# Rows of three tiles projected during the second graph; scores in one ring tile, one exponential for two neighbouring chunks

## The chip, the cores and the metric

The kernel runs on one core of a Trainium2 chip. The core has five engines with a queue each: TensorE (PE, matmuls), VectorE (DVE), ScalarE (ACT, activations such as the exponential), GpSimd (POOL) and SyncE (SP, which here only issues DMA transfers). Each engine takes its instructions in the order of its queue and waits at an instruction until what it needs is there. PE writes its results to banks of PSUM; DVE and ACT read them from there.

The metric is the time of one execution on the device in microseconds (us). The profile comes from one execution of its own.

## The reference, cut to what matters

There are 3327 rows of 256 features, which the kernel pads to 3328: 26 tiles of 128 rows. Two layers follow each other. Each layer first adds a graph operation and then a feed-forward part to `x`. The first layer's feed-forward part is a mixture of experts; the second layer's is causal attention with 4 heads (`nh`) and 4 query experts per head (`ne`). The change is in the second layer:

```python
x = x + L1_gnn(layernorm(x), adj, ...)       # the second graph: softmax over neighbours
x = x + L1_ffn(layernorm(x)[None], ...)[0]   # the attention below

sx = einsum('bsh,ndh->bnsd', x, hl_w) + hl_b[None, :, None, :]
pad = sx == 0
q = einsum('bnsd,neod->bneso', sx, wq)
k = einsum('bnsd,nod->bnso', sx, wk)
v = einsum('bnsd,nod->bnso', sx, wv)
scores = einsum('bnesd,bntd->bnest', q, k) * d ** 0.5 + causal
att = softmax(scores, axis=-1)
qkv = einsum('bnest,bntd->bnesd', att, v)
qkv = where(pad[:, :, None], 0.0, qkv)
gs = softmax(einsum('bnsf,nef->bnse', out, gate_w) + gate_b, axis=-1)
mixed = einsum('bnsed,bnse->bnsd', out, gs)
...                                          # residual, two norms, a small network, a gate
```

## The kernel before

The program has three stages one after the other: the first layer (`graph0` and `Experts`), the second graph (`graph1`), and the attention (`heads`). Every instruction is issued through `InOrder`, which keeps the written order on each engine within one function; that is why the profile gives line 61 for almost all of them, and one goes by the names of tiles.

**The second graph** (`graph1`) goes through blocks of 4 tiles of rows, and within a block through 26 steps, one for each tile of neighbours. A step makes weights (`u`, then `p`) on DVE and ACT and adds four matmuls to the accumulators `acc`. At the start of the next block `finish(t)` divides, adds into `x[:, t, :]`, and stores the tile to `xs` in memory with a DMA that POOL issues. So tiles 0 to 3 of `x` are final from the beginning of the second block on. `heads_fixed` spreads the loads of the attention's weights over the steps of the later blocks (`next(fixed, None)`).

**The attention** (`heads`) starts when the second graph ends. Its unit of work is one tile of query rows `t` and one head `h`; the units run through all heads of a tile and then to the next tile. As the attention is causal, unit `(t, h)` covers the keys of tiles 0 to `t`, cut into `t // 4 + 1` chunks `g` of at most 4 tiles (512 keys): 392 chunks in all. For each chunk:

- `fill` (PE): the scores of the 4 experts, `pqk`, from `qt` and `kt`
- `drain` (DVE): copies them from PSUM to `sc`, and takes the maximum of each row on the way (`mx`); after a unit's last chunk `anmax` is the negative maximum over all its chunks
- `weigh` (ACT): `exp(sc + anmax)` for each expert, and the sum of each row into `den`, one column for each chunk
- `turn` (DVE): transposes blocks of 32 x 32 within `sc`
- `values` (SP): loads the chunk's values `vr` from `vs`
- `attend` (PE): `po` collects `sc` times `vr`

When a unit ends, `over` and `back` take `po` out, and after the fourth head a `tail` is put on a list: it computes the gate, the norms and the small network of that tile in many short steps on POOL, ACT, DVE and PE. `tail` sums `den` over its columns.

`prepare(t, res)` makes what a tile needs: it loads `xres` from `xs`, normalizes (`xn`), turns (`xt`), projects (`psxt`, `sxt`), makes the values `v` and stores them to `vs`, then the keys `kt` (`pk`), the queries (`pq`, into `qt`, for the first five tiles `qts`) and `sx`. It is a generator: each `yield` ends a step, and `run(preps)` takes one step for each tile under way. `nz` and `sxd` mark entries of `sx` that are not zero.

The main loop (lines 1503 to 1531) writes out an order by hand: at chunk `k` it drains as far as `wanted(k)` says (through the whole unit that chunk `k + 2`, or `k + 3`, belongs to), attends chunk `k`, turns the next, issues exponentials of chunks up to `k + 2` or `k + 3` (half of the experts before `back`, half after it, but all after it for a unit's first chunk, when its maximum is young), runs steps of `preps` and `tails`, and fills the next chunk. `sc` comes from a pool of 9 buffers of 4 x 512; the queries of the first five tiles take buffers of the same pool.

Of the kernel before, what the change touches and what calls it, by code (L numbers as in the profile page):

```python
# [12 lines left out]
F32 = mybir.dt.float32  # L13
# [4 lines left out]
AF = mybir.ActivationFunctionType  # L18
# [4 lines left out]
P = 128  # L23
# [78 lines left out]
class Net:  # L102
# [378 lines left out]

        return beside

    def graph1(self, xs, made, pool):
        tc, a, x = self.tc, self.a, self.x
        nc = InOrder(tc)
        fixed = self.heads_fixed(pool, nc)
        HP = NP // 2

        PARTS = ((0, HP, HP + 9 * P, NP), (0, HP, NP))  # L490
        with ExitStack() as ctx:
# [125 lines left out]
            first.close()  # L617

            ep = ctx.enter_context(tc.tile_pool(name="g1e", bufs=4))
            abp = ctx.enter_context(tc.tile_pool(name="g1ab", bufs=2))  # L620
            psa = ctx.enter_context(tc.tile_pool(name="g1acc", bufs=8, space=PSUM))
            blocks = [range(i, min(i + 4, NT)) for i in range(0, NT, 4)]
# [123 lines left out]
            weights(0)  # L746
            weights(1)
            masked(0)
            for k, (b, j) in enumerate(steps):

                if b > 2:
                    next(fixed, None)
                if k + 8 in when:
                    load(*when[k + 8])
                if k + 2 < len(steps):
                    if steps[k + 2][1] % 4 == 0 and groups:
                        panel(*groups.pop(0))
                    weights(k + 2)
                if k + 3 in when:
                    sign(*when[k + 3])  # L760
                if k + 1 < len(steps):
                    masked(k + 1)
                gather(k)
                if b and 1 <= j <= len(blocks[b - 1]):
                    finish(blocks[b - 1][j - 1])
                if k in when:
                    top(*when[k], PARTS[1])
                if b + 1 < len(blocks):
                    if j == 16:
                        dg = shifts(b + 1)  # L770
                    if j == 18:
                        pb = rows(b + 1, dg)
                    if j == 21:
                        spread_rows(b + 1, pb)
            for t in blocks[-1]:
                finish(t)


    def heads_fixed(self, one, nc):

# [75 lines left out]
    def heads(self, xs, vs, out):  # L856
# [3 lines left out]
        with ExitStack() as ctx:  # L860
            one = ctx.enter_context(tc.tile_pool(name="at", bufs=1))
            self.work = ctx.enter_context(tc.tile_pool(name="atw", bufs=2))
            scp = ctx.enter_context(tc.tile_pool(name="ats", bufs=9))
            vrp = ctx.enter_context(tc.tile_pool(name="atv", bufs=3))
            tl = ctx.enter_context(tc.tile_pool(name="att", bufs=2))
            sm = ctx.enter_context(tc.tile_pool(name="atsm", bufs=4))
# [5 lines left out]
            )  # L872

            kt = one.tile([P, 4, NP], F32, name="kt")


            load = dict(act=0.0, dve=0.0)
# [29 lines left out]

            def prepare(t, res):

                x = tl.tile([P, D], F32, tag="xres", name="xres", bufs=2)  # L910
                nc.sync.dma_start(out=x, in_=xs[ts(t, P), :])
                yield
# [25 lines left out]
                xt = self.work.tile([P, 2, P], F32, tag="xt", name="xt2", bufs=1)  # L938
                turned(xn, xt)
                yield  # L940
                pp = ps.tile([P, 2, P], F32, tag="b", name="psxt")
                for c in range(2):
                    for k in range(2):
                        nc.tensor.matmul(
                            pp[:, c, :], hlt[:, k, ts(c, P)], xt[:, k, :], start=(k == 0), stop=(k == 1)
                        )
                sxt = self.work.tile([P, 2, P], F32, tag="sxt", name="sxt")
                for c in range(2):
                    nc.scalar.activation(
                        sxt[:, c, :], pp[:, c, :], AF.Identity, bias=hlb[:, c : c + 1]  # L950
                    )
                nz = self.work.tile([P, 2, P], F32, tag="xn", name="nz", bufs=1)
                nonzero(nz, sxt)
                load["act"] += 0.6
                yield

                pp = ps.tile([P, 4, 64], F32, tag="b", name="pv")
                for c in range(2):
                    nc.tensor.matmul(
                        pp[:, 2 * c : 2 * c + 2, :], sxt[:, c, :], wv[:, c, :], start=True, stop=True  # L960
                    )
                v = self.work.tile([P, 4, 64], F32, tag="v", name="v", bufs=1)
                empty(v, pp, D)
                yield

                sxd = self.work.tile([P, 4, P], F32, tag="sxd", name="sxd", bufs=3)
                for k in range(2):
                    for s in range(2):
# [9 lines left out]
                        )  # L978
                for s in range(2):
                    empty(kt[:, s::2, ts(t, P)], pp[s], D)  # L980
                for b in range(4):
                    nc.sync.dma_start(
                        out=vs[:, :, 4 * t + b, :].rearrange("h r d -> r h d"),
                        in_=v[ds(Q * b, Q), :, :],
                    )
                yield
                if t < AHEAD:

                    qt = scp.tile([P, 4, BLK], F32, tag="sc", name="qts")[:, :, : 2 * P]
                    qt = qt.rearrange("p h (i q) -> p h i q", i=2)  # L990
                else:
                    qt = tl.tile([P, 4, 2, P], F32, tag="qt", name="qt")
# [9 lines left out]
                for s in range(2):  # L1002
                    empty(qt[:, s::2, :, :], pp[s], BLK, 8.0)
                yield
                sx = tl.tile([P, D], F32, tag="sx", name="sx", bufs=5)
                turned(sxt.rearrange("p c q -> p (c q)"), sx.rearrange("p (c q) -> p c q", c=2))
                res.update(sx=sx, sxd=sxd, qt=qt)

# [47 lines left out]

            def drain(u, g):

                n = span(u["t"], g)[1] * P
                last = g == u["t"] // 4  # L1060
                if g == 0:
                    u["sc"] = {}
                    u["mx"] = sm.tile([P, 4, 8], F32, tag="mx", name="mx")
                sc = u["sc"][g] = scp.tile([P, 4, BLK], F32, tag="sc", name="sc")
                for e in range(4):
                    s, m = u["pq"][e][:, :n], u["mx"][:, e, g : g + 1]
                    if last:
                        nc.vector.tensor_tensor_reduce(
                            sc[:, e, :n], s, mask[:, BLK - n :], 1.0, NEG, ALU.add, ALU.max, m
                        )  # L1070
                    else:
                        nc.vector.tensor_scalar(
                            sc[:, e, :n], s, 1.0, None, ALU.mult, ALU.max, accum_out=m
                        )
                    load["dve"] += 0.12 + 0.00104 * n
                if last:
                    u["nmax"] = sm.tile([P, 4], F32, tag="nmax", name="anmax")
                    nc.vector.tensor_reduce(
                        u["nmax"], u["mx"][:, :, : g + 1], AX.X, ALU.max, negate=True
                    )  # L1080
                    load["dve"] += 0.2

            def weigh(u, g, experts):

                n = span(u["t"], g)[1] * P
                q = ready[u["t"]]
                if u["h"] == g == 0 and 0 in experts:
                    q["den"] = sm.tile([P, 16, 7], F32, tag="den", name="aden", bufs=3)
                for k in experts:
                    e = u["sc"][g][:, k, :n]  # L1090
                    nc.scalar.activation(
                        e, e, AF.Exp, bias=u["nmax"][:, k : k + 1],
                        accum_out=q["den"][:, 4 * u["h"] + k, g : g + 1],
                    )
                    load["act"] += 0.26 + 0.00088 * n
# [8 lines left out]
            def turn(u, g):  # L1104


                n = span(u["t"], g)[1] * P
                w = u["sc"][g][:, :, :n]
                nc.vector.transpose(w, w)
                load["dve"] += 0.1 + 0.00417 * n  # L1110

# [331 lines left out]
                nc.sync.dma_start(out=out[ts(t, P), :], in_=fo)  # L1443

            units = [dict(t=t, h=h) for t in range(NT) for h in range(4)]
            chunks = [(u, g) for u in units for g in range(u["t"] // 4 + 1)]
            def begin(u):

                t = u["t"]
# [46 lines left out]
            drain_to(wanted(0))  # L1496
            for k in range(2):
                values(*chunks[k])
                weigh(*chunks[k], range(4))
            turn(*chunks[0])  # L1500
            fill_next()
            ended, flipped, weighed = None, 1, 2
            for k, (u, g) in enumerate(chunks):
                drain_to(wanted(k))
                attend(u, g)
# [3 lines left out]
                if k + 2 < len(chunks):  # L1509
                    values(*chunks[k + 2])  # L1510
                rest = []
                while weighed < min(k + 3 + extra(k), len(chunks)):
                    c = chunks[weighed]
                    if c[1]:
                        weigh(*c, range(2))
                    rest.append((*c, range(2 if c[1] else 0, 4)))
                    weighed += 1
                if ended:
                    back(ended)
                last = u if g == u["t"] // 4 else None  # L1520
# [17 lines left out]
class Experts:  # L1538
# [97 lines left out]
    def bank(self):  # L1636
        return self.ps.tile([P, 2, D], F32, tag="r", name="rbank")
# [355 lines left out]
def tile_adj_ffn_d2(ctx: ExitStack, tc: tile.TileContext, a: dict, out: bass.AP):  # L1993
# [5 lines left out]
    with tc.tile_pool(name="feat", bufs=1) as fp:  # L1999
# [4 lines left out]
        with ExitStack() as rows:  # L2004
            with ExitStack() as moe:
                experts = Experts(moe, net, dram, fp)
                net.graph0(experts, weights)
                experts.run(net.graph1_rows(rows))
            net.graph1(xs, experts, ctx.enter_context(tc.tile_pool(name="atf", bufs=1, side="right")))
    net.heads(xs, vs, out)  # L2010


# [76 lines left out]
```

## Time and profile before

| | us |
|---|---|
| median of 3 runs (2863.0 to 2865.1) | 2863.1 |
| the profiled execution | 2863.9 |
| its span, first to last instruction | 2862.2 |
| last `p` of the second graph starts | 961.1 |
| first scores `pqk` of the attention start | 977.9 |
| first maximum `anmax` of tile 1 ends | 1010.5 |
| first maximum of tile 4 ends | 1077.4 |
| first maximum of tile 8 ends | 1248.2 |
| first maximum of tile 16 ends | 1779.9 |
| first maximum of tile 25 ends | 2711.1 |

The attention takes two thirds of the time. Some groups of instructions in it, by form, from 1200 us to the end (count, mean of one in us):

| instruction | count | mean |
|---|---|---|
| ACT exponential of 512, `sc<-sc,anmax` | 946 | 0.713 |
| ACT exponential of 384 | 464 | 0.606 |
| DVE transpose of 4 x 512 | 237 | 2.305 |
| DVE transpose of 4 x 384 | 116 | 1.773 |
| DVE drain of 512, with maximum | 652 | 0.680 |
| DVE drain of 512, with mask and maximum | 288 | 0.680 |

In lines that list instructions in order of time, the columns are: start, duration, engine, line, operation, tile written and tiles read, shapes, how many in a row, and in brackets the idle time of the engine before it with what ended it. `PEld` is the weight load of PE. A chain of waits follows the work that ended last back from the end; its shares are shares of the span.

### The profile page before, as it was taken

What the parts mean: (1) busy time and instruction counts of PE and PEld (TensorE: products, weight loads), DVE (VectorE), ACT (ScalarE), POOL (GpSimd) and SP (SyncE); (2) the same over time, 40 slices, a digit from 0 to 9 for tenths busy, and PEclk for the clock granted to TensorE, in tenths of its full rate; (3) what the DMA queues carried; (4) which work ended last, traced back from release to release, by engine and by line L of the source; (5) the groups of instructions that cost most, each with busy time, mean ns of one, the idle gap of its engine ahead of it and who ended that gap; (6) DMA issues with size and microseconds to landing.
All of it is one profiled execution on the core that took longest, in us unless ns stands there. A gap on an engine that the chain in (4) does not pass through costs nothing.

```text
span 2862.2 us, 125012 instructions
## 1 busy us (share of the span) xinstructions
PE 2665.0 (93%) x53422; PEld 1979.1 (69%) x53422; DVE 2368.9 (83%) x5525; ACT 1790.0 (63%) x5130; POOL 1075.3 (38%) x1562
## 2 busy tenths in 40 slices
PE   7999988878989899999999999999999999999995
PEld 5888877756767666676666666666666666666664
DVE  5203643589999588899999999999999999999996
ACT  6510135555555367777777777777777777777774
POOL 5541644532132137755444333333233222223122
PEclk9999999999999799999999999999999999999998
DMA  9994568657775232333433443434343444434332
GB/s 381 388 337 138 180 217 266 209 183 247 275 273 180 73 94 84 109 108 116 116 111 113 119 121 114 116 118 121 114 127 116 120 120 119 123 116 122 117 107 78
DMA packets 258188, 449.69 MB, mean 157 GB/s; under 512 B 58816, under 2 KB 156608, under 8 KB 257504
## 3 DMA queue, kind: packets, MB, share of 16 engines
q1 hardware_dynamic: 245536, 417.50, 46.0%
q0 software_dynamic: 6576, 18.02, 1.7%
q8 instruction: 420, 6.88, 1.0%
q10 hardware_dynamic: 5520, 6.18, 0.6%
q14 instruction: 136, 1.11, 0.1%
HBM read 393.37 MB, written 25.88 MB: 146 GB/s over the span
## 4 chain that ended last, share of the span: by engine, by line
DVE 35%; PE 28%; ACT 3%; issue 2%; POOL 1%; DMA 0%; SPq 0%; POOLq 0%; DVEq 0%; ACTq 0%
DVE sc L61 32%; PE pqk L61 10%; PE po L61 10%; PE acc L61 2%; ACT sc L61 2%; PE ptO L61 2%; PE psxt L61 1%; PE pt L61 1%; PE pq L61 1%; PE ph L61 0%; ACT sq L61 0%; PE pk L61 0%; PE pv L61 0%; DVE anmax L61 0%; DVE gl L61 0%
## 5 line engine op out<-in xcount | busy, mean ns | idle before, releaser
L61 ACT ACTIVATE sc<-sc,anmax 128x512 f32<-128x512 f32 (+3 forms) x1568 | 1041.4, 669 | 102.9 <-DVE anmax L61 102.9
L61 PEld LDWEIGHTS po<-sc,vr 32*64 32x64 f32 x43728 | 662.5, 131 | 299.1 <-issue 147.6
L61 DVE STREAM_TRANSPOSE sc<-sc 128x2048 f32<-128x2048 f32 (+3 forms) x392 | 816.0, 2082 | 9.7 <-ACT sc L61 9.4
L61 PE MATMUL po<-sc,vr 32*64 32x128 f32 x43728 | 761.1, 276 | 31.6 <-DVE sc L61 21.5
L61 PE MATMUL pqk<-kt,qt 64*128 64x512 f32 (+1 forms) x2944 | 764.4, 585 | 19.0 <-DVE fgs L61 6.6
L61 DVE TENSOR_SCALAR_CACHE_REDUCE sc<-pqk 128x512 f32<-128x512 f32 (+2 forms) x1152 | 653.1, 621 | 26.0 <-PE pqk L61 23.8
L61 PEld LDWEIGHTS pqk<-kt,qt 64*128 64x128 f32 x2944 | 315.9, 185 | 239.5 <-issue 80.9
L61 PE MATMUL acc<-wh,p 128*128 128x259 f32 x1352 | 309.2, 386 | 35.6 <-DVE p L61 35.6
L61 PEld LDWEIGHTS acc<-wh,p 128*128 128x128 f32 x1352 | 253.2, 190 | 93.4 <-DVE p L61 53.3
L61 PE MATMUL acc<-y,pan 128*128 128x256 f32 x1352 | 298.4, 382 | 1.7 <-issue 1.7
L61 ACT ACTIVATION_READ_ACCUMULATOR sc<-sc,anmax 128x1 f32 x1568 | 299.5, 191 | 0.0
L61 PEld LDWEIGHTS acc<-y,pan 128*128 128x128 f32 x1352 | 257.2, 191 | 38.7 <-issue 3.2
L61 POOL TENSOR_TENSOR ot<-ot,sxd 128x512 f32<-128x512 f32 x83 | 105.9, 1276 | 436.2 <-ACT ot L61 431.1
L61 DVE CUSTOM_DVE_ANT_0 sc<-pqk,mask 128x512 f32<-128x512 f32 (+3 forms) x416 | 241.9, 636 | 25.4 <-PE pqk L61 24.6
L61 ACT ACTIVATE u<-u,d 128x512 f32<-128x512 f32 (+1 forms) x182 | 125.2, 688 | 159.2 <-DVE u L61 159.1
L61 DVE SCALAR_TENSOR_TENSOR u<-bc,d 128x512 f32<-128x512 f32 (+1 forms) x182 | 136.0, 748 | 0.1
L61 DVE SCALAR_TENSOR_TENSOR p<-pan,u 128x512 f32<-128x512 f32 (+1 forms) x182 | 126.1, 693 | 10.3 <-PE acc L61 6.1
L61 ACT COPY qkv<-ptO 128x272 f32<-128x272 f32 x104 | 39.7, 381 | 131.0 <-PE ptO L61 130.8
L61 PE MATMUL ptO<-igw,ot 128*128 128x68 f32 x832 | 115.7, 282 | 3.8 <-DVE sc L61 2.1
L61 PEld LDWEIGHTS ptO<-igw,ot 128*128 128x128 f32 x832 | 101.5, 192 | 22.5 <-issue 15.2
L61 ACT ACTIVATE junk<-ar 128x1664 bf16<-128x1664 f32 x52 | 82.8, 1592 | 54.1 <-DMA ar<-in_adj_dram 53.6
L61 DVE CUSTOM_DVE_ANT_0 sg<-sg,dst 128x1664 bf16<-128x1664 bf16 (+2 forms) x56 | 100.1, 1796 | 1.2 <-ACT dst L61 1.0
(356 smaller groups left out, 3082.0 us busy)
## 6 DMA issues: line engine op xcount, KB each, us to landing
vr<-vs SPq DMA_DIRECT2D x976, 128.0 KB
ar<-in_adj_dram SPq DMA_DIRECT2D x104, 832.0 KB
vr<-vs SPq DMA_DIRECT2D x544, 96.0 KB
pan<-in_adjt_dram SPq DMA_DIRECT2D x156, 256.0 KB
pan<-in_adjt_dram SPq DMA_DIRECT2D x26, 1024.0 KB
pan<-in_adjt_dram SPq DMA_DIRECT2D x20, 832.0 KB
w1e<-w SPq DMA_DIRECT2D x59, 256.0 KB
took<-places SPq DMA_DIRECT2D x59, 129.0 KB
```

The source lines that it names most:

```text
L61: made = make(*args, **kw)
```

## The change

It has two parts, and several edits that go with them.

**Rows of tiles 0 to 2.** In `graph1` a new generator `early(t)` runs for tiles 0, 1 and 2, begun at steps 110, 115 and 136 of 182, one of its steps in each step of the graph. It takes `x[:, t, :]` from where it lies, normalizes it (statistics on DVE, the rest on POOL), turns, projects and makes the values, with accumulator banks of `graph1`, and stores the values to `vs`. `sxt` stays in a pool that both functions share, with three buffers. In `heads`, `prepare` of these tiles goes straight to `heads_of`, the part from `nz` and the keys on. `projected`, `valued` and `keep_values` are the former lines of `prepare` as functions. `sx` has 4 buffers in place of 5.

**Scores in a ring, exponentials in pairs.** The pool of 9 buffers becomes one tile `ring` of 4 x (9 x 512), and chunk `c` lies in slot `c % 9` (`c % 6` for the first 24 chunks, while the last three slots hold the queries of the first five tiles). Two neighbouring chunks `g` and `g + 1` of one unit are a pair when `g` is even and they lie in neighbouring slots; a first chunk that is shorter than 512 is then put at the end of its slot, so that the two touch. `weigh` makes one exponential for an expert over both chunks, with one sum, in the column of `g`; `den` is cleared on POOL when a tile begins, because columns of second chunks are no longer written. There are 150 pairs. In the main loop a pair advances `weighed` by two, and a pair that is not a unit's first may be begun one step early, with two of its experts.

```diff
+            def early(t):
+                mv = s.tile([P, 2], F32, tag="mv", name="mv", bufs=6)
+                rs = s.tile([P, 2], F32, tag="rs", name="rs", bufs=6)
+                st = s.tile([P, 6], F32, tag="bnst", name="bnst")
+                nc.vector.bn_stats(st, x[:, t, :])
+                nc.vector.bn_aggr(mv, st)
+                yield
+                nc.gpsimd.tensor_scalar(rs[:, 0:1], mv[:, 1:2], 1e-5, None, ALU.add)
+                nc.gpsimd.tensor_tensor(rs[:, 0:1], rs[:, 0:1], self.nhalf[:, :1], ALU.pow)
+                xn = eap.tile([P, D], F32, tag="xn", name="xn3")
+                nc.gpsimd.tensor_tensor(xn, x[:, t, :], mv[:, 0:1].to_broadcast([P, D]), ALU.subtract)
+                nc.gpsimd.tensor_tensor(xn, xn, rs[:, 0:1].to_broadcast([P, D]), ALU.mult)
+                yield
+                yield
+                pt = bank()
+                for c in range(2):
+                    nc.tensor.transpose(pt[:, c, :], xn[:, ts(c, P)], self.ident)
+                xt = eap.tile([P, 2, P], F32, tag="xt", name="xt3")
+                nc.scalar.copy(xt, pt)
+                yield
+                sxt = pool.tile([P, 2, P], F32, tag="sxt", name="sxt", bufs=3)
+                self.sxts.append(sxt)
+                self.projected(nc, t, bank, sxt, xt)
+                yield
+                pv = self.valued(nc, bank, sxt)
+                v = eap.tile([P, D], F32, tag="v", name="v3")
+                nc.scalar.copy(v.rearrange("p (c q) -> p c q", c=2), pv)
+                self.keep_values(nc, vs, t, v)
+
+            begin = {4 * NT + 6: 0, 4 * NT + 11: 1, 5 * NT + 6: 2}
+            begun = []
             for k, (b, j) in enumerate(steps):
                 if b > 2:
                     next(fixed, None)
+                if k in begin:
+                    begun.append(early(begin[k]))
+                begun = [e for e in begun if next(e, e) is None]
...
             def prepare(t, res):
+                if t < len(self.sxts):
+                    yield from heads_of(t, res, self.sxts[t])
+                    return
...
+            RING = 9
+            ring = one.tile([P, 4, RING * BLK], F32, name="ring")
...
             def drain(u, g):
+                c = u["c"] + g
                 n = span(u["t"], g)[1] * P
+                at = slot(c) * BLK + (BLK - n if paired(c) else 0)
...
-                sc = u["sc"][g] = scp.tile([P, 4, BLK], F32, tag="sc", name="sc")
+                sc = u["sc"][g] = ring[:, :, ds(at, n)]
+                u["at"][g] = at
...
-            def weigh(u, g, experts):
+            def slot(c):
+                return c % (RING if c >= 24 else 6)
+            def paired(c):
+                u, g = chunks[c]
+                return g % 2 == 0 and g < u["t"] // 4 and slot(c) + 1 == slot(c + 1)
+            def weigh(c, experts):
+                u, g = chunks[c]
                 n = span(u["t"], g)[1] * P
+                if paired(c):
+                    n += span(u["t"], g + 1)[1] * P
                 q = ready[u["t"]]
                 if u["h"] == g == 0 and 0 in experts:
                     q["den"] = sm.tile([P, 16, 7], F32, tag="den", name="aden", bufs=3)
+                    nc.gpsimd.memset(q["den"], 0.0)
                 for k in experts:
-                    e = u["sc"][g][:, k, :n]
+                    e = ring[:, k, ds(u["at"][g], n)]
                     nc.scalar.activation(
                         e, e, AF.Exp, bias=u["nmax"][:, k : k + 1],
                         accum_out=q["den"][:, 4 * u["h"] + k, g : g + 1],
                     )
...
                 rest = []
-                while weighed < min(k + 3 + extra(k), len(chunks)):
-                    c = chunks[weighed]
-                    if c[1]:
-                        weigh(*c, range(2))
-                    rest.append((*c, range(2 if c[1] else 0, 4)))
-                    weighed += 1
+                until = min(k + 3 + extra(k), len(chunks))
+                while weighed < until:
+                    left = range(begun, 4)
+                    if chunks[weighed][1]:
+                        half = len(left) // 2
+                        weigh(weighed, left[:half])
+                        left = left[half:]
+                    rest.append((weighed, left))
+                    weighed += 2 if paired(weighed) else 1
+                    begun = 0
+                if weighed < len(chunks) and chunks[weighed][1] and paired(weighed) and not begun:
+                    if not rest or rest[0][1][0] > 1:
+                        weigh(weighed, range(1))
+                        rest.append((weighed, range(1, 2)))
+                        begun = 2
```

## The prediction

> **What bounds the kernel now.** I read the page's busy shares and its chain first, then the busy time by stretches, then the order of time at the three places that the change touches.
>
> ```profile
> PE 2665.0 (93%) x53422; PEld 1979.1 (69%) x53422; DVE 2368.9 (83%) x5525; ACT 1790.0 (63%) x5130; POOL 1075.3 (38%) x1562
> ...
> DVE 35%; PE 28%; ACT 3%; issue 2%; POOL 1%; DMA 0%; SPq 0%; POOLq 0%; DVEq 0%; ACTq 0%
> ```
>
> ```profile
> 970.00:985.00 15.00, 13.09 (x87) 10.96 (x94) 6.17 (x32) 6.96 (x30) 1.10 (x1) 0.50 0.17 40
> 985.00:1010.00 25.00, 16.41 (x148) 12.97 (x147) 6.07 (x26) 6.03 (x20) 5.71 (x8) 0.50 0.21 56
> 1010.00:1120.00 110.00, 101.87 (x2068) 77.32 (x2055) 94.96 (x276) 77.16 (x265) 57.91 (x80) 1.00 0.32 91
> 2200.00:2600.00 400.00, 395.65 (x11484) 268.64 (x11485) 395.70 (x834) 298.12 (x937) 109.99 (x152) 1.00 0.41 120
> ```
>
> The columns are length, then busy time of PE, weight load, DVE, ACT and POOL, the granted clock, and DMA. From 970 to 1010 (rows of tiles 0 and 1 are prepared there) DVE works 12.2 of 40 us: a chain of small steps, each waiting for the one before, at half the PE clock. From about 1200 on DVE is full: 395.7 of 400 us. ACT has a quarter of its time free, and the view of who waits for whom says that DVE hardly waits for it (from 1010 to 2846):
>
> ```profile
> DVE sc L61 <- PE pqk L61: 44.2, 50, 4.5
> DVE sc L61 <- ACT sc L61: 9.2, 8, 3.6
> ```
>
> So shorter ACT work alone can give back 9.2 us at most, and work that makes DVE wait for ACT costs directly.
>
> **The change, part by part.** The sum is made against the profiled execution, 2863.9 us (span 2862.2); the median of the runs is 2863.1, so no correction.
>
> *Rows of tiles 0 to 2 are projected earlier (gain).* The start of the third stage, in order of time:
>
> ```profile
> 964.45 0.33 SPq L61 DMA_DIRECT2D xres<-xs  x1
> ...
> 977.89 5.00 PE L61 MATMUL pqk<-kt,qts 64*128 64x128 f32 x32 [0.19 <-ACT qts L61]
> ...
> 987.50 0.16 DVE L61 TENSOR_REDUCE anmax<-mx 128x4 f32<-128x4 f32 x1
> ...
> 1010.38 0.16 DVE L61 TENSOR_REDUCE anmax<-mx 128x4 f32<-128x4 f32 x1
> ```
>
> Tile 0: loading, normalizing, turning, projecting and making values fill 964.5 to 974.2. What is left (pk, pq) needs its weights and the banks that the last finish frees at 964.8, but the copies into kt wait for the last store of x, because kt lies where x lay. In the changed order POOL does nz (1.10) and the memset of den before the two last stores, so these issue until about 966.4; a load of the same 128 KB took 964.45 to 966.50, 2.05 us, so they land at 968.4. Copy 0.4, copy into qt 0.7, and scores begin near 969.9, not 977.9: 8 us. Tile 1: from its predecessor's last maximum (987.66) to its own first (1010.54) are 22.9 us. Afterwards ptO 2.2, pq 1.9, two copies 1.1, first scores 1.25 and four drains 1.6 remain, 8.1: 14.8 us. Together 23. Bounds: 15, if kt and sxd arrive as late as half of that, and 30, if tile 2 gains as well (its pv, sxt and norm go too).
>
> *The same work inside the second graph (cost).* Three times: statistics 0.41 + 0.18 on DVE, about 97% busy there (48.5 of 50 us from 850 to 900): 1.8 us. On PE turning, projecting and values, 0.4 + 1.1 + 0.7, hidden while DVE is the bound, but tile 2's fall after 900, where PE is 48.4 of 50 busy: 2.2, half hidden. Four stores of values per tile stand in SP's queue behind the copy that they need and ahead of panel loads; a load leads its use by 8 steps of some 2 us, which covers a wait of 2 to 4. POOL's subtraction and multiplication (0.6 each) lie in idle time, and so do four ACT instructions per tile. Sum 3, bounds 0 and 6.
>
> *The memset of den on POOL (cost).* A merged exponential leaves entries of den unwritten, so each tile's den is cleared on POOL, behind all that POOL has queued, and the tile's first exponential waits for it. Behind that exponential stand all of ACT's queue, DVE's transpose, and PE's po. Tile 2 before:
>
> ```profile
> 1029.92 0.61 ACT L61 ACTIVATE sc<-sc,anmax 128x384 f32<-128x384 f32 x1
> ...
> 1031.23 0.22 POOL L61 TENSOR_TENSOR gss<-gss,gsm 128x16 f32<-128x16 f32 x1
> ...
> 1031.82 1.91 POOL L61 TENSOR_TENSOR qkv<-qkv,gss 128x1024 f32<-128x1024 f32 x1
> ...
> 1032.45 1.78 DVE L61 STREAM_TRANSPOSE sc<-sc 128x1536 f32<-128x1536 f32 x1
> ...
> 1035.98 0.73 POOL L61 TENSOR_TENSOR fx<-fx,sx 128x256 f32<-128x256 f32 x1
> ```
>
> In the changed order the memset stands right behind this last addition. It ends at 1036.7; clearing 128x112 is about 0.2 (128x128 took 0.20); four exponentials of 0.6 follow, and the transpose of 1032.45 starts near 1039.6, 7.2 late. The same sum gives 7.9 for tile 3 (addition ends 1062.75), 7.7 for tile 4 (1087.03), 4.1 for tile 5 (1124.4, behind lnb): 27. For tiles 6 to 8, 15 and 21 to 23 POOL is 1.0 to 1.8 late, about 8 more; elsewhere it is done 1 to 11 us early. I take 24 of the 27, since ACT, DVE and PE all stand in order behind it; bounds 12 (POOL's tail work also shrinks when tiles 0 and 1 move closer, and DVE has gaps there) and 30.
>
> *One exponential for two chunks (gain and cost).* 600 of 1568 exponentials go. One of 512 takes 0.713, one of 384 0.607: 0.106 for 128 elements, so 0.28 is fixed, and ACT saves 168 us. DVE's part of that is at most the 9.2 above; I take 3, bounds 0 and 9. Against it: the maximum of a unit (one tile and head) releases its exponentials, and DVE covers them with one transpose and one drain. A unit in full flow:
>
> ```profile
> 2415.86 0.18 DVE L61 TENSOR_REDUCE anmax<-mx 128x4 f32<-128x24 f32 x1
> ...
> 2416.07 0.61 ACT L61 ACTIVATE sc<-sc,anmax 128x384 f32<-128x384 f32 x1 [5.56 <-DVE anmax L61]
> ...
> 2418.48 0.71 ACT L61 ACTIVATE sc<-sc,anmax 128x512 f32<-128x512 f32 x1
> ...
> 2420.06 1.77 DVE L61 STREAM_TRANSPOSE sc<-sc 128x1536 f32<-128x1536 f32 x1
> ```
>
> The four exponentials of the first chunk end 1.6 before the transpose that needs them. With the second chunk in them they take 4 x 0.42 = 1.7 longer: 0.1 short, with the handing over 0.2. I did this for the 81 units whose first two chunks are merged (slack of the first transpose against 1.3 or 1.7): 15 have room, 33 lack 0.26 on average, and 33 lack 1.1, because ACT began late behind a copy that waits for PE. Together 45 us, and 8 for POOL's later lateness, 53. The short ones land on a DVE that is 99% busy; the long ones where PE is late anyhow and DVE would next wait for scores (44.2 us in all). I take half, 26; bounds 8 and 53. Later pairs begin an expert or two a step ahead and have room.
>
> *Nothing:* the transposes, now 4 x 512 with a stride: 4x128, 4x256 and 4x384 took 0.70, 1.24 and 1.77, a line that meets 2.30 at 2048, as the flat ones took. The ring has as many buffers as the pool, and the changed order has no new wait on them.
>
> Sum: 2863.9 - 23 + 3 + 24 + 26 - 3 = 2891.
>
> The row on the clock: PE was granted 0.50 from 970 to 1010, after waits of up to 5 us, and eight psxt matmuls took 2.08 at 970.46 against 1.11 at 1028.20. [...]
>
> **The rivals.** (a) Faster: the waits for ACT are absorbed. DVE stands before scores for 44.2 us already; if PE is the true bound there, later transposes only use these gaps. For it: PE is 93% busy. Against: 395.7 of 400 us of DVE. With the low bounds, 12 and 8, and the gain of 6 on ACT: 2863.9 - 23 + 3 + 12 + 8 - 6 = 2858, and with the start's 30, 2851. It decides when the two costs together come to less than 17 to 20 us. (b) Everything passes: 2863.9 - 18 + 5 + 30 + 45 = 2926. For it: three engines wait in order. Against: gaps of PE at the very units that lack most. (c) Start and costs cancel: the two costs at 17 to 29 in all, 2858 to 2870. (d) The early rows bring nothing, because the stage starts when x has been stored: 10 us instead of 23, 2904, inside the forecast's range.
>
> **How the numbers follow.** Forecast (2870 to 2912, (d) included) 0.55; (b) and above 0.15; (c) 0.10; (a) 0.20. A measurement of this kernel can tell about 0.2%, 5.7 us, from no change: faster 0.20, same 0.10, slower 0.70. All low bounds give 2845, all high ones 2938; 8 in 10 is 2857 to 2920; the forecast's own range is 2870 to 2912.
>
> **What would show it.** Right: first scores near 970 and tile 1's first maximum 20 to 25 us earlier; ACT waiting for POOL's memset for 4 to 8 us at each of tiles 2 to 5; DVE's wait for ACT up from 9 to 50 or more; ACT's busy time down by some 170 with the end not earlier. Wrong: POOL ahead of the exponentials at tiles 2 to 5, or a DVE whose wait for scores falls by as much as its wait for ACT grows.

## The result, and the profile after

The changed kernel takes 2949.4 us (median of 5 runs, 2945.1 to 2955.0) against 2863.0: 1.0304 times as long, 95% interval 1.0289 to 1.0318. That is 86 us more; the forecast was 28 more, its range ended at 2912, and the wider one (8 in 10) at 2920.

Two lines of the page after, busy times first and then the chain of work that ended last:

```profile
PE 2707.3 (92%) x53422; PEld 1997.5 (68%) x53422; DVE 2377.7 (81%) x5521; ACT 1622.4 (55%) x3931; POOL 1080.1 (37%) x1591
...
PE 29%; DVE 26%; ACT 12%; issue 2%; POOL 2%; DMA 1%; SPq 1%; POOLq 0%; DVEq 0%; ACTq 0%
```

ACT has 167.6 us less to do (1790.0 before), just what 600 exponentials at 0.28 come to. DVE's work is nearly as before (2368.9). And yet ACT's share of the chain went from 3% to 12%: an engine that is idle 45% of the time holds the others up.

The stretches of time that were shown of before, with the same columns (length, busy PE, weight load, DVE, ACT, POOL, granted clock, DMA):

```profile
970.00:985.00 15.00, 12.22 (x124) 10.19 (x126) 8.74 (x43) 7.00 (x30) 2.29 (x3) 0.54 0.29 70
985.00:1010.00 25.00, 24.69 (x408) 18.72 (x406) 21.04 (x75) 15.39 (x56) 3.29 (x7) 0.94 0.35 93
1010.00:1120.00 110.00, 86.21 (x1587) 62.77 (x1587) 71.38 (x197) 56.18 (x174) 52.04 (x73) 0.84 0.24 67
2200.00:2600.00 400.00, 387.66 (x10824) 258.84 (x10811) 378.33 (x810) 249.57 (x637) 109.90 (x157) 0.98 0.40 114
```

From 985 to 1010 DVE now works 21.0 of 25 us (6.1 before): the gain at the start is there. From 1010 to 1120 it works 71.4 of 110 (95.0 before), and PE's granted clock is 0.84 in place of 1.00. From 2200 to 2600 it works 378 of 400 where it worked 396: a smaller loss that goes on to the end. Who DVE waits for, from 1010 on (total, times, longest):

```profile
DVE ring L61 <- ACT ring L61: 85.6, 66, 9.9
DVE ring L61 <- PE pqk L61: 71.5, 73, 6.1
```

Before these were 9.2 and 44.2. The wait for ACT grew by 76, and the wait for PE didn't shrink in exchange: it grew by 27.

Two places show how these waits come about. The first is tile 2's beginning, where the first head's maximum ended at 1005.9. Its lines in order of time, from the second head's maximum on:

```profile
1010.41 0.16 DVE L61 TENSOR_REDUCE anmax<-mx 128x4 f32<-128x4 f32 x1
...
1014.09 0.72 POOL L61 TENSOR_TENSOR fx<-fx,sx 128x256 f32<-128x256 f32 x1
1014.75 0.19 POOL L61 MEMSET aden<- 128x112 f32 x1
1014.98 0.61 ACT L61 ACTIVATE ring<-ring,anmax 128x384 f32<-128x384 f32 x1 [6.81 <-POOL aden L61]
...
1017.51 1.78 DVE L61 STREAM_TRANSPOSE ring<-ring 128x1536 f32<-128x1536 f32 x1 [6.93 <-ACT ring L61]
...
1017.80 1.91 PE L61 MATMUL pqk<-kt,ring 64*128 64x384 f32 x4 [5.17 <-ACT qkv L61]
```

Read from the brackets: ACT stood 6.81 us for the clear, DVE 6.93 for ACT's exponentials, and PE 5.17 for a copy (`qkv`) that stands behind those exponentials on ACT and frees a bank. Three engines stood for a clear of 0.19 us that stood itself behind POOL's work of the tile before. The second place is a unit in full flow, the same one (tile 22, third head) that the prediction showed:

```profile
2488.77 0.18 DVE L61 TENSOR_REDUCE anmax<-mx 128x4 f32<-128x24 f32 x1
...
2488.98 1.04 ACT L61 ACTIVATE ring<-ring,anmax 128x896 f32<-128x896 f32 x1 [7.16 <-DVE anmax L61]
...
2492.07 1.03 ACT L61 ACTIVATE ring<-ring,anmax 128x896 f32<-128x896 f32 x1
...
2493.23 1.78 DVE L61 STREAM_TRANSPOSE ring<-ring 128x1536 f32<-128x1536 f32 x1 [0.17 <-ACT ring L61]
```

From the maximum to the fourth exponential's start are 3.1 us, three merged ones; the transpose waits 0.17, the small shortage that the prediction had worked out for this unit.

Where the loss arises along the way, by the end of each tile's first maximum against before: tile 2 -21.8, tile 5 +5.6, tile 9 +28.0, tile 16 +46.0, tile 25 +83.6. This run was already 3.5 ahead of the profile of before when the first early row began, so 18 of the 21.8 are the change's: the start gains nearly as forecast (20). Tiles 2 to 5 lose 27, tiles 5 to 9 another 22, and the rest 56. Two suspects were open for the last two: the clear (once a tile) and the merged first chunks (four times a tile).

### The profile page after: what moved, and what is told of

The parts are those of the page before. It is cut to its first block, busy times and chain, and to the rows that moved or that the text cites. A ratio compares the mean times of both kernels' runs of the same rounds, so it can differ in the third digit from the quotient of the medians.

```text
span 2948.5 us, 123806 instructions
## 1 busy us (share of the span) xinstructions
PE 2707.3 (92%) x53422; PEld 1997.5 (68%) x53422; DVE 2377.7 (81%) x5521; ACT 1622.4 (55%) x3931; POOL 1080.1 (37%) x1591
## 3 DMA queue, kind: packets, MB, share of 16 engines
q14 instruction: 126, 1.03, 0.1%
## 4 chain that ended last, share of the span: by engine, by line
PE 29%; DVE 26%; ACT 12%; issue 2%; POOL 2%; DMA 1%; SPq 1%; POOLq 0%; DVEq 0%; ACTq 0%
DVE ring L61 23%; PE po L61 10%; ACT ring L61 10%; PE pqk L61 10%; PE acc L61 3%; PE ptO L61 2%; ACT sq L61 1%; PE pq L61 1%; PE ph L61 1%; POOL fx L61 1%; SPq L61 1%; POOL qkv L61 1%; DVE p L61 1%; PE pt L61 0%; PE psxt L61 0%
## 5 line engine op out<-in xcount | busy, mean ns | idle before, releaser
L61 ACT ACTIVATE ring<-ring,anmax 128x896 f32<-128x896 f32 (+7 forms) x968 | 873.6, 907 | 187.1 <-DVE anmax L61 153.0
L61 DVE STREAM_TRANSPOSE ring<-ring 128x2048 f32<-128x2048 f32 (+3 forms) x392 | 816.1, 2083 | 89.2 <-ACT ring L61 88.6
L61 PEld LDWEIGHTS po<-ring,vr 32*64 32x64 f32 x43728 | 677.5, 133 | 310.3 <-issue 130.6
L61 PE MATMUL pqk<-kt,qt 64*128 64x512 f32 (+1 forms) x2944 | 789.1, 595 | 51.3 <-DVE ring L61 7.8
L61 PE MATMUL po<-ring,vr 32*64 32x128 f32 x43728 | 777.3, 280 | 33.6 <-DVE ring L61 18.1
L61 DVE TENSOR_SCALAR_CACHE_REDUCE ring<-pqk 128x512 f32<-128x512 f32 (+2 forms) x1152 | 654.4, 622 | 53.6 <-PE pqk L61 52.1
L61 DVE CUSTOM_DVE_ANT_0 ring<-pqk,mask 128x512 f32<-128x512 f32 (+3 forms) x416 | 241.8, 636 | 22.6 <-PE pqk L61 22.4
L61 ACT ACTIVATION_READ_ACCUMULATOR ring<-ring,anmax 128x1 f32 x968 | 185.0, 191 | 0.0
L61 ACT COPY ot<-po 128x512 f32<-128x512 f32 x83 | 47.9, 577 | 116.9 <-PE po L61 116.8
```

The lines of the kernel that those rows point to most:

```text
L61: made = make(*args, **kw)
```

## The experiments

All of them are edits of the changed kernel. As runs of before differ a little from batch to batch (2862.2 to 2868.2), the last column is the ratio applied to 2863.1; the intervals make a difference between two rows uncertain by about 5 to 7 us, and by more for `x2_no_first_pair`.

| kernel | what of the change is in it | median us | ratio to before (95%) | us against before |
|---|---|---|---|---|
| changed | all | 2949.4 | 1.0304 (1.0289 to 1.0318) | +87 |
| `x9_ring_only` | ring | 2865.9 | 0.9995 (0.9986 to 1.0003) | -1 |
| `x3_no_pairs` | ring, early rows | 2843.4 | 0.9927 (0.9910 to 0.9944) | -21 |
| `x4_clear_no_pairs` | ring, early rows, clear | 2883.0 | 1.0070 (1.0053 to 1.0086) | +20 |
| `x8_first_pairs_only` | ring, early rows, first pairs | 2878.8 | 1.0062 (1.0045 to 1.0079) | +18 |
| `x5_both` | ring, early rows, later pairs | 2888.9 | 1.0087 (1.0066 to 1.0109) | +25 |
| `x7_copies_first` | the same, another order on ACT | 2882.8 | 1.0075 (1.0059 to 1.0092) | +21 |
| `x1_clear_early` | all, but the clear a tile earlier | 2896.2 | 1.0108 (1.0091 to 1.0125) | +31 |
| `x2_no_first_pair` | all but first pairs | 2928.8 | 1.0224 (1.0190 to 1.0258) | +64 |
| `x6_two_for_one` | as `x1_clear_early`, exponentials not merged | 3007.1 | 1.0507 (1.0487 to 1.0527) | +145 |
| `x10_change_without_early_rows` | all but early rows | 2974.8 | 1.0378 (1.0362 to 1.0394) | +108 |

"First pairs" are those of a unit's chunks 0 and 1, "later pairs" those of 2 and 3, 4 and 5. Where a pair is in a kernel without "clear" in the list, `den` is cleared a tile earlier; `x3_no_pairs` has no clear at all. Up to tile 11 the early clear costs 2 us at most: with only later pairs, which begin at tile 12, the first maxima stay at -23.8 to -23.9 from tile 3 to tile 11, and without clear and pairs they go from -23.9 to -25.7.

### The clear a tile earlier

```diff
-                res.update(sx=sx, sxd=sxd, qt=qt)
+                den = sm.tile([P, 16, 7], F32, tag="den", name="aden", bufs=4)
+                nc.gpsimd.memset(den, 0.0)
+                res.update(sx=sx, sxd=sxd, qt=qt, den=den)
 ...
-                if u["h"] == g == 0 and 0 in experts:
-                    q["den"] = sm.tile([P, 16, 7], F32, tag="den", name="aden", bufs=3)
-                    nc.gpsimd.memset(q["den"], 0.0)
```

> The changed kernel with one thing taken back: den of a tile is cleared when its queries are prepared, about a tile before its first exponential, so no exponential waits for POOL behind the tile before. Theory A (the clear costs at tiles 2 to 5 only, the steady loss of 3.4 us a tile later comes from the merged first chunks): 27 us less than the changed kernel's 2949, about 2922, with the first maxima level again from tile 2 to tile 5 and the same slope after tile 9. Rival B (the clear, once a tile, makes the loss of all tiles): nearly all 86 us come back, 2850 to 2870.

Neither: 53 us come back by the medians, 56 by the ratios, twice what theory A had and two thirds of what rival B had. The first maxima are level from tile 2 (-17.8) to tile 4 (-18.3), and a loss of 2.3 us a tile on average remains, to +29.6 at tile 25.

### No merged first chunks

```diff
-                return g % 2 == 0 and g < u["t"] // 4 and slot(c) + 1 == slot(c + 1)
+                return g % 2 == 0 and 0 < g < u["t"] // 4 and slot(c) + 1 == slot(c + 1)
```

> The changed kernel with the first two chunks of a unit no longer merged (pairs begin at the third chunk); the clear stays where the change put it. Theory A: the steady loss after tile 5 goes, 55 to 78 us, to 2871 to 2894; DVE's wait for ACT's exponentials back from 88 to 10 to 35 us. Rival B (the clear makes it): 2940 to 2950. Rival C (later pairs, or the ring, make it): also 2935 and above, but then with DVE waiting at the second or third transpose of a unit.

Theory A missed by 35 us and more. Only 23 us of the 87 go (by the ratios), so first pairs aren't all of the steady loss; rivals B (2940 to 2950) and C (2935 and above) stood too high. DVE's wait for ACT halved (88.3 to 44.0, from 980 on), but its wait for PE's scores rose from 73.1 to 92.2.

### No pairs and no clear

```diff
-                return g % 2 == 0 and g < u["t"] // 4 and slot(c) + 1 == slot(c + 1)
+                return False
 ...
-                    nc.gpsimd.memset(q["den"], 0.0)
```

> No exponentials merged and no clear; what is left of the change is the early rows of tiles 0 to 2 and the ring. Theory A: the gain at the start alone, 22 less and 5 more in the second graph, so 2841 to 2850. Rival C (the ring's strided tiles cost): above 2863, with a slope over the tiles though nothing is merged.

As theory A had it: 2843.4, and the first maxima keep their distance from tile 3 (-23.9) to tile 24 (-24.1). DVE's waits in it, from 1010 on:

```profile
DVE ring L61 <- PE pqk L61: 45.2, 54, 4.9
DVE ring L61 <- ACT ring L61: 9.7, 8, 2.9
```

These are the waits of before (44.2 and 9.2). This kernel is the yardstick for the rest, and it beats both kernels.

### Only later pairs, the clear early

This is the first two edits together.

> Both of the first two edits: den cleared a tile earlier, and the first two chunks not merged; later pairs stay merged. Theory A: the costs add, 86 less 27 and 55 to 78, so 2845 to 2868. Rival C (later pairs cost as well): 2880 and above. Theory A's weakest point is whether the two costs are the same time counted twice: then it stands no lower than the better of the two single edits.

Rival C is right in this: later pairs cost as well, 46 us over no pairs. DVE's wait for ACT is no larger than without pairs (10.6), but that for PE's scores is 78.9 in place of 45.2. One place where it arises, tile 24's second head, in order of time:

```profile
2639.01 1.11 PE L61 MATMUL ptO<-igw,ot 128*128 128x68 f32 x8
...
2641.48 1.03 ACT L61 ACTIVATE ring<-ring,anmax 128x896 f32<-128x896 f32 x1
...
2642.50 1.03 ACT L61 ACTIVATE ring<-ring,anmax 128x896 f32<-128x896 f32 x1
...
2643.53 0.36 ACT L61 COPY qkv<-ptO 128x272 f32<-128x272 f32 x1
...
2643.94 0.91 PE L61 MATMUL pqk<-kt,qt 64*128 64x384 f32 x2 [2.35 <-ACT qkv L61]
...
2644.89 0.56 DVE L61 TENSOR_SCALAR_CACHE_REDUCE ring<-pqk 128x384 f32<-128x384 f32 x1 [2.34 <-PE pqk L61]
```

`ptO` is ready at 2640.1, but its copy starts at 2643.5, behind two exponentials of 1.03. PE needs the bank that the copy frees, and DVE needs the scores. Without pairs the same copy started 1.2 after `ptO`, and PE waited 0.17:

```profile
2605.62 1.11 PE L61 MATMUL ptO<-igw,ot 128*128 128x68 f32 x8
...
2607.96 0.36 ACT L61 COPY qkv<-ptO 128x272 f32<-128x272 f32 x1
...
2608.38 0.91 PE L61 MATMUL pqk<-kt,qt 64*128 64x384 f32 x2 [0.17 <-ACT qkv L61]
```

Over the whole attention PE waits for ACT's copies into `ot` 11.4 us here (none without pairs), into `qkv` 6.8 (1.1 without) and into `sx` 5.9 (1.5 without). That gave theory D: the place in ACT's order costs. The runs that follow test it and price the parts.

### The clear alone

```diff
-                return g % 2 == 0 and g < u["t"] // 4 and slot(c) + 1 == slot(c + 1)
+                return False
```

> No exponentials merged, but the clear of den on POOL ahead of each tile's first exponential, as in the change: the price of the clear by itself, against 2843 for the kernel with neither. By the prediction's sum (27 raw at tiles 2 to 5, 8 at later ones) 24 to 35 more, 2867 to 2878. By the difference of the two kernels without merged first chunks (2929 with the clear in its place, 2889 with it a tile earlier) 40 more, 2883. If the clear costs only together with merged exponentials: below 2860.

41 us by the ratios, the second number. All of it arises at tiles 2 to 8: against no clear the first maxima lose 6.9, 12.5, 10.0 and 3.8 in the course of tiles 2 to 5, then 4.0, 3.1 and 2.2, and little after that. Tile 3's wait and what follows it:

```profile
1045.99 0.72 ACT L61 ACTIVATE ring<-ring,anmax 128x512 f32<-128x512 f32 x1 [8.11 <-POOL aden L61]
...
1049.24 3.78 PE L61 MATMUL pqk<-kt,ring 64*128 64x512 f32 x6 [5.74 <-ACT qkv L61]
...
1061.12 3.91 PE L61 MATMUL pqk<-kt,ring 64*128 64x512 f32 x8
```

The last line's eight matmuls took 2.36 at the same place without the clear. The stretches around it, with the granted clock third from the end:

```profile
1061.00:1065.00 4.00, 4.00 (x15) 1.60 (x14) 1.58 (x7) 3.77 (x11) 1.07 (x1) 0.50 0.02 4
1065.00:1069.00 4.00, 4.00 (x133) 3.70 (x134) 3.97 (x7) 0.86 (x3) 0.00 (x0) 1.00 0.08 20
```

PE is granted 0.50 from 1045 to 1065 and 1.00 from there to 1075; from 1075 to 1084, where it stops again, the mean is 0.89. Between 1055 and 1065 DVE works 5.4 of 10 us while PE works all of them at 0.50: there PE sets the pace. That tile 3 loses 12.5, where ACT's wait is 8.1, fits this, but no run has these waits at full clock.

### Two exponentials for one, in the changed order

```diff
-                    e = ring[:, k, ds(u["at"][g], n)]
-                    nc.scalar.activation(
-                        e, e, AF.Exp, bias=u["nmax"][:, k : k + 1],
-                        accum_out=q["den"][:, 4 * u["h"] + k, g : g + 1],
-                    )
+                    lo = u["at"][g]
+                    for j in range(2 if paired(c) else 1):
+                        m = span(u["t"], g + j)[1] * P
+                        e = ring[:, k, ds(lo, m)]
+                        lo += m
+                        nc.scalar.activation(
+                            e, e, AF.Exp, bias=u["nmax"][:, k : k + 1],
+                            accum_out=q["den"][:, 4 * u["h"] + k, g + j : g + j + 1],
+                        )
```

> The kernel with den cleared a tile earlier (2896) in the same order, but each merged exponential issued as the two that it replaces, one right behind the other: the order of the change without the merging. Theory D (what costs is the place in ACT's order: two chunks' exponentials ahead of the first transpose and of the copies into ot and qkv, for which PE waits): no better than 2896, and by 0.28 for each of 600 more instructions worse where nothing covers them, 2900 to 2930. Rival E (the wide instruction itself costs, a reader must wait for both chunks): 2843 to 2865.

Here, too, `den` is cleared a tile earlier. Rival E is out, and theory D's number was too small: 3007, 114 us more than merged by the ratios. With 600 x 0.28 = 168 us more on ACT, two thirds of them pass. So merging as such helps in this order, by 114 us; the order is what costs. DVE's waits (from 980 on):

```profile
DVE ring L61 <- PE pqk L61: 132.3, 111, 7.9
DVE ring L61 <- ACT ring L61: 78.1, 72, 2.7
```

The order without pairs issues as many exponentials of the same lengths and takes 2843.

### Later pairs behind the copies

```diff
-                    if chunks[weighed][1]:
+                    if chunks[weighed][1] and not paired(weighed):
                         half = len(left) // 2
 ...
-                if weighed < len(chunks) and chunks[weighed][1] and paired(weighed) and not begun:
-                    if not rest or rest[0][1][0] > 1:
-                        weigh(weighed, range(1))
-                        rest.append((weighed, range(1, 2)))
-                        begun = 2
```

> den cleared a tile earlier, first two chunks not merged, and of the later pairs all four exponentials issued behind the copies into qkv and ot of the same step, none ahead of them and none a step early. Theory D: the 45 us that later pairs cost against no pairs (2889 against 2843) go for the most part, 2843 to 2865, and PE's wait for ACT's ot and qkv goes from 18 us to below 6. Rival E: 2885 or more. A third way: the copies are in time, but the last two experts' exponentials then end behind the transpose that needs them, seen as DVE waiting for ACT's exponentials 30 us or more.

The third way. PE's wait for `qkv` is 5.8 and that for `ot` 0.3, and DVE's wait for scores is back at 40.4; but DVE now waits 49.5 for ACT, at the third chunk's transpose: against no pairs the third chunks lose 46 us over tiles 12 to 25, and the others win a little of it back. A place in tile 22:

```profile
2376.47 0.59 ACT L61 COPY ot<-po 128x512 f32<-128x512 f32 x1 [2.87 <-PE po L61]
...
2377.64 1.16 ACT L61 ACTIVATE ring<-ring,anmax 128x1024 f32<-128x1024 f32 x1
...
2381.05 1.14 ACT L61 ACTIVATE ring<-ring,anmax 128x1024 f32<-128x1024 f32 x1
...
2382.31 2.31 DVE L61 STREAM_TRANSPOSE ring<-ring 128x2048 f32<-128x2048 f32 x1 [1.81 <-ACT ring L61]
```

Four exponentials of 1.15 last from 2377.6 to 2382.2, and the transpose needs only the first half of each. Ahead of the copies they keep PE waiting, behind them DVE. At this place there is room between the two for one chunk's exponentials (4 x 0.71), not for two. In all, this order (+21) costs about as much as the other (+25).

### First pairs alone

```diff
-                return g % 2 == 0 and g < u["t"] // 4 and slot(c) + 1 == slot(c + 1)
+                return g == 0 < u["t"] // 4 and slot(c) + 1 == slot(c + 1)
```

> den cleared a tile earlier, and only the first two chunks of a unit merged, later ones not. The first chunks' own price: if it is what the trace of the kernel with all pairs shows at the first transposes (48 of 53 us), 2843 plus 45 to 50, 2888 to 2893. If the prices of first and later pairs add (2896 with all pairs less 2889 with later ones), 2850. My prediction's own number was 26, with 53 as the upper bound: 2869 to 2896.

39 us by the ratios: more than my 26 (half of 53, of which 8 were for the clear), less than the 45 to 50 read from the trace with all pairs, and far from 7. Its waits from 1010 on, to be set against those without pairs:

```profile
DVE ring L61 <- ACT ring L61: 48.0, 61, 4.4
DVE ring L61 <- PE pqk L61: 41.4, 43, 6.2
```

The wait for ACT grew by 38.3, the wait for PE fell by 3.8. So nearly nothing of the late transposes landed in gaps that PE leaves. First pairs alone (39) and later pairs alone (46) come to 52 together, not 85.

### The ring alone, and the change without early rows

```diff
-            begin = {4 * NT + 6: 0, 4 * NT + 11: 1, 5 * NT + 6: 2}
+            begin = {}
```

Together with the edit of "no pairs and no clear" this is the first, by itself the second.

> The changed kernel without early rows, without merged exponentials and without the clear: what is left is scores in the ring, read and written with a stride. If the ring costs nothing, as the prediction had it, 2860 to 2867, and the 21 us that the kernel without pairs gained (2843) are the early rows' alone. If the strided reads or the ring's order cost something that the early rows made good, 2870 or more; if the ring gained, 2855 or less.

> The whole change but for the early rows. If the parts add: the change's 2949 and the 18 to 21 us of the early rows, 2967 to 2970. If the early rows make the clear dearer, because tile 2 comes sooner while POOL's work behind tiles 0 and 1 takes as long as before, the sum stands lower: 2950 to 2962.

The ring costs nothing (0.9986 to 1.0003), so the early rows alone are 19 us of the 21. The first maxima of this run stay 3.5 to 3.7 us behind those of before from tile 1 to tile 24, as far as this run lay behind when the attention began. Taken from the whole change they are 21 (108 less 87): the parts add here. The 2975 lies above the expected 2967 to 2970 because the runs of before stood 5 us higher in that batch.

## Why the prediction was wrong

The direction was right, the size was not. The forecast's terms beside what the runs put in their place, by the ratios:

| term | forecast | measured |
|---|---|---|
| early rows, start and second graph | -23 + 3 | -19 to -21 |
| the clear | +24 | +41 alone, +56 beside pairs |
| first chunks merged | +26 | +39 |
| later chunks merged | 0 | +46 alone, +13 beside first pairs |
| relief on ACT | -3 | none seen |
| ring, transposes with a stride | 0 | -1 (-4 to +1) |
| sum | +27, to 2891 | -21 + 39 + 13 + 56 = +87 |

Some 60 us are missing in the forecast: by this order of adding up 32 are the clear's, 13 each the first and the later pairs', and 3 the relief that didn't show. As the costs of the clear and the pairs don't add, another order would share them out otherwise.

**Early rows: right.** From the last `p` of the second graph to tile 2's first maximum are 43.3 us after and 66.6 before: 23.3, forecast 23. Tile 0's first scores begin at 972.4, which is 7.1 earlier counted from the last `p`, and not 8: POOL issued the last store at 967.27, not at 966.4, it ended at 970.7 (968.4), and the copy into `kt` waited for it; 1.6 of these 2.3 us are the later end of the second graph. The steps of the second graph from the first early row on take 5 us longer, not 3.

**The clear: the mechanism was right, 24 was too small, and so was its upper bound of 30.** Forecast for tiles 2 to 5 were 7.2, 7.9, 7.7 and 4.1; measured in the kernel with the clear alone were 6.9, 12.5, 10.0 and 3.8. Tiles 2 and 5 fit. At tiles 3 and 4 PE is granted 0.50 for about 16 and 8 us of work after the wait, which the sum left out; how much of their 6.9 us more is the clock alone was not tried. Tiles 6 to 8, whose lateness of 1 to 1.8 each I had moved into another term and halved, lost 9.3: ACT waits there 1.2 to 1.5 for the clear, and the granted clock is 0.91 on average from 1120 to 1200 and 0.98 from 1200 to 1400 (0.96 and 1.00 in the kernel before). Beside all pairs the clear costs 15 more. Most of it arises late: at tiles 21 to 23 the first exponential starts 1.3 to 2.2 us after its maximum without pairs, which costs nothing there, and 2.2 to 3.5 with them, and from tile 20 to 25 the first maxima fall back by 11 us against the kernel with pairs and an early clear. It takes the first pairs for this: from tile 2 to tile 25 the first maxima lose 42 to the clear without pairs, 44 beside later pairs alone (`x2_no_first_pair` against `x5_both`) and 58 beside all. That the first transpose has more room without merging would explain it; that was not tried apart.

**First pairs: "I take half, 26" is the step that failed first.** The shortage of 45 was of the right size. That half of it would land in DVE's waits for scores was argued from 44.2 us of such waits; with first pairs alone these fell by 3.8 and DVE's waits for ACT rose by 38.3. So the waits for scores took up next to nothing of what the late transposes lost.

**Later pairs: "Later pairs begin an expert or two a step ahead and have room" failed outright.** I looked only at the transposes, for which it holds (DVE waits 10.6 for ACT with later pairs alone). What they cost is what stands behind them on ACT: the copies of `qkv`, `ot` and `sx`, for which PE waits, and after it DVE. Issued behind the copies they cost the transposes instead.

**Relief on ACT.** Its busy time fell by the 168 forecast, and no kernel with merged exponentials came below the one without. So no run shows that the 9.7 us that DVE waits for ACT without pairs can be had by giving ACT less to do.

**The rivals.** (b), "everything passes", had the right mechanism, and its price of 2926 was 23 short: its clear of 30 was 26 too small and the later pairs' 13 were not in it, while its first pairs (45) and its start (-18 and +5) were 6 and 8 too dear. (a) rested on PE's gaps taking up the waits; DVE's wait for PE grew by 27 instead. (c) fell with the size of the costs, and (d) with the start, which gave 23 and not 10. The signs named were there: tile 1's first maximum 20.9 earlier, first scores at 972.4, ACT waiting for POOL at tiles 2 to 5 (6.8, 8.1, 8.7 and 2.9), 76 us more of DVE waiting for ACT, and no earlier end.

**The clock.** In the kernel with the clear alone PE stopped at 1011.2, 1043.5 and 1080.5 and was granted 0.50 within 1 to 3 us, while it still waited (5.2, 5.7 and 7.1 in all). A shorter pause came before a fall, too: in the kernel before, PE paused for 1.13 us until 1122.3, and from 1123 to 1126 the granted clock is 0.50. Not every such pause did: after one of 2.01 us until 1474.9 in the kernel before, the granted clock stays 1.00 (1472 to 1480). After the three long waits PE worked at 0.50 for about 4, 16 and 8 us before 1.00 was granted. Tiles 2 to 5 lost 33.2 where the sum's raw number was 27; no run shows how much of these 6 us the clock is.

## What beats both kernels

`x3_no_pairs`, the early rows with the ring but without pairs and clear: 2843.4 us, 0.9927 of before. Its busy times and chain:

```profile
PE 2651.7 (93%) x53422; PEld 1968.1 (69%) x53422; DVE 2372.8 (84%) x5521; ACT 1791.1 (63%) x5131; POOL 1076.2 (38%) x1565
...
DVE 34%; PE 33%; ACT 3%; issue 2%; DMA 1%; POOL 1%; SPq 1%; DVEq 0%; POOLq 0%; ACTq 0%
```

ACT has 169 us more to do than in the changed kernel, and 3% of the chain instead of 12%.

## What to carry to other kernels

Joining two instructions on an engine with idle time need not save anything (600 exponentials fewer cost 52 us here, with the clear early), and the joined instruction gives its first result later (1.03 us in place of 0.60) and holds back all that is queued behind it: look at what waits for its first half, and at each copy behind it that frees a buffer. An instruction of 0.2 us on the critical path costs the backlog of the queue it is put in (ACT stood 6.8 us at tile 2 for a clear of 0.19), so a clear belongs where its engine has time, a tile ahead of its use. Before halving a cost because another engine has gaps, check that those gaps come right after the delay; and price edits one at a time, as the prices of two that delay the same queue need not add (39 and 46 came to 52).

## What the runs showed of the hardware

- In the kernel before, a pause of PE of 1.13 us was followed by a granted clock of 0.50 from 1123 to 1126; after one of 2.01 us until 1474.9 it stayed at 1.00 (1472 to 1480). After waits of 5.2, 5.7 and 7.1 us at tiles 2, 3 and 4 in the kernel with the clear alone PE worked at 0.50 for about 4, 16 and 8 us before it was granted 1.00. Why 16, in a stretch in which it never paused, no run here shows.
- A merged exponential took 0.26 to 0.28 us less than its two parts: 128x896 took 1.03 where 128x384 and 128x512 took 0.60 and 0.71, and 128x1024 took 1.14 to 1.16 where two of 128x512 took 1.42.
- Reading and writing scores at a stride in one large tile cost nothing that the runs show: 4 x 512 transposes took 2.305 us as before, and the kernel with the ring alone took 0.9995 (0.9986 to 1.0003) of the time before.
